# Rebuilding the opening of a fused graph-layer kernel: loads on one queue, a new product order, and the work around it moved

## The chip, the cores and the metric

The kernel runs on one core of one Trainium2 chip. The metric is the device time of one execution in microseconds (us); four executions of the kernel before lie within 1.4 us.

## The reference

For each of 64 batches of 256 tokens of width 768: a layer norm, then a graph layer over a 0/1 adjacency. In short (zero biases and the relation terms as in the full text):

```python
h    = max(layernorm(x), 0)                       # 64 x 256 x 768
adj  = heads.astype(float);  radj = adj.swapaxes(1, 2)
ctx  = (adj @ (h @ Wadj.T + badj)) / deg  + (radj @ (h @ Wrev.T + brev)) / rdeg
ctx += h @ Wself.T + bself
rel  = agg @ Wr.T + br*deg + ragg @ Wrr.T + brr*rdeg    # sums of relation embeddings
out  = x + ctx + rel
```

## The kernel before

A step t does the large products of batch M = t, the aggregates (adjacency times normalised tokens) of batch A = t+1, and the statistics and normalising of batch N = t+2. The products use a bilinear scheme with 15 products instead of 18: each is a sum of blocks of the left operand (made on POOL, GpSimd) times a sum of weight blocks (made once, on DVE, VectorE), and is added to one or more outputs. Several products accumulate in one PSUM bank (x, y, z, w), and DVE adds the bank into the output *in between*: so the next product of that bank must wait until DVE has read it.

```python
ORDER = (    # (product, bank, bias row, adds into x, left sums made on POOL just before)
    (11, "w", ...), (10, "z", ...), (3, "w", 1, ...), (2, "z", 0, ...), (5, "y", ...), (9, "x", ...),
    (7, "v", ...), (8, "y", ...), (6, "x", ...), (15, "u", ...), (14, "y", 2, ...), (12, "x", 4, ...),
    (4, "t", ...), (13, "y", 3, ...), (1, "x", 5, ...))
AHEAD = ("b2-a1", "a1+b1", "a2+b2")             # left sums made at the end of the step before

def normalise(b):                               # hx and lo on DVE, hi on ACT (ScalarE)
    ...
    for c in range(C):                          # C = 2 halves
        nc.vector.tensor_scalar(hx[:, c, :], s["x"][:, c, :], mean, 0.0, op0=ALU.subtract, op1=ALU.max)
        nc.scalar.activation(s["hi"][:, c, :], hx[:, c, :], AF.Copy, scale=rstd)
        nc.vector.scalar_tensor_tensor(s["lo"][:, c, :], hx[:, c, :], rstd, s["hi"][:, c, :], ...)

def step(t):
    M, A, N = t, t + 1, t + 2
    load(N)                                     # x, adj, xT of batch t+2, on SP's queue
    for k, (n, bank, row, reads, needs) in enumerate(ORDER):     # k: the "place" in the step
        for name in needs: combine_left(M, name)                 # POOL
        if t == 0 and k + 3 < len(ORDER): combine_weights(ORDER[k + 3][0])
        product(M, n, banks[bank], start, row)                   # PE (TensorE)
        for read in reads: add_out(M, banks[bank], *read)        # DVE
        if k in (1, 2, 3, 4, 5, 6): aggregate(A, k - 1)          # PE, then a multiply on DVE
        if k == 5: self_features(A)                              # POOL
        if k == 6: degrees(N); statistics(N)                     # ACT, DVE
        if k == 9: spread(N)
        if k == 11: normalise(N)
        if k == 13: store first half of out[M]
    for name in AHEAD: combine_left(A, name)                     # POOL
    store second half of out[M]
```

Each engine is given its instructions in the order of this loop, so "place" below always means: after the product with that number k, from 0 to 14, in this loop. (Cuts: reads and needs of ORDER, conditions at the ends.)

## Time and profile before

| | before |
|---|---|
| time, median (4 runs) | 2993.8 us |
| span of the profiled run | 2992.0 us, clock 0.994 |
| PE busy | 2911.9 us, 97% |
| first product of step 0 / of step 1 | 84.73 / 139.85 us |
| steps 1 to 62, apart | 45.25 us each |

PE is full from 140 us on. The prediction shows the lines for that.

### The profile page before, as it was taken

To read this page: it belongs to the slowest core of one execution; us is meant where nothing else is said; L and a number is where in the kernel's file an instruction comes from. 1 tells how busy PE (TensorE), PEld (TensorE's weight loads), DVE (VectorE), ACT (ScalarE), POOL (GpSimd) and SP (SyncE) were. 2 spreads that over 40 slices of the span, in tenths; PEclk is the share of its full clock that TensorE was granted. 3 is DMA by queue.
4 is the path that set the end of the run, shared out by engine and by line. 5 is a ranking of instruction groups with operands and counts; after the bars stand their busy time and mean duration, and the time that the engine had idled before them with its cause. 6 is when DMAs were issued, how large, how long until landed. Compare 5 with 4: busy or idle time off the path is not lost.

```text
span 2992.0 us, 33451 instructions
## 1 busy us (share of the span) xinstructions
PE 2911.9 (97%) x13514; PEld 2533.5 (85%) x13514; DVE 1243.4 (42%) x2530; ACT 355.3 (12%) x838; POOL 1779.5 (59%) x905
## 2 busy tenths in 40 slices
PE   2899999999999999999999999999999999999999
PEld 1688888888888888888888888888888888888887
DVE  3743434444444444443443444444444344444431
ACT  1111110110110111111111111111101101101100
POOL 2575565575565565665665665665755655755654
PEclk9899999999999999999999999999999999999999
DMA  7122222222222222122122122122122222222210
GB/s 233 63 72 74 88 68 75 78 72 79 74 75 81 71 77 81 64 85 81 64 82 84 64 76 91 64 74 92 64 74 84 71 75 76 73 81 74 75 64 22
DMA packets 126054, 233.27 MB, mean 78 GB/s; under 512 B 7092, under 2 KB 68276, under 8 KB 125896
## 3 DMA queue, kind: packets, MB, share of 16 engines
q1 hardware_dynamic: 114136, 219.28, 21.3%
q10 hardware_dynamic: 11760, 11.80, 1.3%
q8 instruction: 109, 1.79, 0.2%
q14 instruction: 49, 0.40, 0.0%
HBM read 180.46 MB, written 50.59 MB: 77 GB/s over the span
## 4 chain that ended last, share of the span: by engine, by line
PE 96%; DVE 1%; POOL 1%; ACTq 1%; DMA 1%; ACT 0%; issue 0%; SPq 0%; POOLq 0%
PE y L345 22%; PE x L345 22%; PE pa L319 12%; PE w L345 11%; PE z L345 11%; PE t L345 5%; PE u L345 5%; PE v L345 5%; ACTq L154 1%; POOL xT L310 1%; PE y L350 1%; PE x L350 0%; DVE w L180 0%; PE w L350 0%; PE z L350 0%; PE pt L272 0%
## 5 line engine op out<-in xcount | busy, mean ns | idle before, releaser
L340 POOL TENSOR_TENSOR b0+b<-X 128x768 f32<-128x768 f32 x64 | 118.2, 1847 | 736.7 <-PE z L345 736.7
L345 PE MATMUL y<-w,X 128*128 128x256 f32 x2304 | 530.8, 380 | 2.5 <-DVE x L358 2.5
L345 PEld LDWEIGHTS y<-w,X 128*128 128x128 f32 x2304 | 433.8, 190 | 66.9 <-DVE x L358 2.9
L310 POOL TENSOR_TENSOR xT<-xT,row 128x1536 f32<-128x1536 f32 x128 | 443.5, 3465 | 44.1 <-DMA row<-d 39.1
L319 PE MATMUL pa<-a,hi 128*128 128x512 f32 x768 | 352.4, 459 | 32.5 <-ACT hi L297 28.7
L340 POOL TENSOR_TENSOR X<-X 128x768 f32<-128x768 f32 x192 | 349.5, 1820 | 12.0 <-PE y L345 7.0
L345 PE MATMUL x<-w,X 128*128 128x256 f32 x1536 | 352.5, 379 | 0.0
L345 PE MATMUL x<-w,a2+b 128*128 128x256 f32 x1536 | 352.3, 379 | 0.0
L324 DVE TENSOR_TENSOR X<-pa,row 128x512 f32<-128x512 f32 x384 | 265.5, 692 | 187.4 <-PE pa L319 181.8
L345 PEld LDWEIGHTS x<-w,X 128*128 128x128 f32 x1536 | 287.0, 190 | 40.7
L345 PEld LDWEIGHTS x<-w,a2+b 128*128 128x128 f32 x1536 | 287.1, 190 | 38.1
L319 PE MATMUL pa<-a,lo 128*128 128x512 f32 x768 | 306.4, 399 | 0.5 <-DVE lo L298 0.5
L311 ACT ACTIVATE X<-xT 128x1536 f32<-128x1536 f32 x64 | 95.2, 1488 | 1599.2 <-POOL xT L310 1599.2
L340 POOL TENSOR_TENSOR a2+b<-X,a2+b 128x768 f32<-128x768 f32 x128 | 233.1, 1821 | 1.6 <-PE x L345 1.6
L319 PEld LDWEIGHTS pa<-a,hi 128*128 128x128 f32 x768 | 146.4, 191 | 61.3 <-ACT hi L297 29.6
L298 DVE SCALAR_TENSOR_TENSOR lo<-hx,cols,hi 128x768 fp32r<-128x768 f32 x128 | 130.4, 1019 | 161.7 <-ACT hi L297 161.7
L297 ACT ACTIVATE hi<-hx,cols 128x768 fp32r<-128x768 f32 x128 | 119.9, 937 | 563.3 <-DVE hx L294 563.3
L340 POOL TENSOR_TENSOR a2+b<-X 128x768 f32<-128x768 f32 x64 | 116.3, 1817 | 117.3 <-PE x L350 117.3
L340 POOL TENSOR_TENSOR a1+a<-X 128x768 f32<-128x768 f32 x64 | 116.9, 1826 | 106.8 <-PE w L350 106.8
L345 PE MATMUL w<-w,X 128*128 128x256 f32 x768 | 177.8, 381 | 0.0
L345 PE MATMUL w<-w,a1+b 128*128 128x256 f32 x768 | 176.3, 379 | 0.9 <-DVE x L360 0.9
L345 PE MATMUL t<-w,X 128*128 128x256 f32 x768 | 176.1, 379 | 0.7 <-DVE w L177 0.7
(84 smaller groups left out, 4008.7 us busy)
## 6 DMA issues: line engine op xcount, KB each, us to landing
x<-in_x_dram SPq DMA_DIRECT2D x64, 768.0 KB, 7.1
xT<-in_x_t_dram SPq DMA_DIRECT2D x64, 768.0 KB, 4.7
out_dram<-x SPq DMA_DIRECT2D x128, 384.0 KB, 3.1
adj<-in_adj_dram SPq DMA_DIRECT2D x64, 512.0 KB
row<-d SPq DMA_DIRECT2D x64, 512.0 KB
w<-in_Wself_dram ACTq DMA_DIRECT2D x6, 768.0 KB
w<-in_Wrev_dram ACTq DMA_DIRECT2D x5, 768.0 KB, 8.7
w<-in_Wadj_dram ACTq DMA_DIRECT2D x4, 768.0 KB, 10.3
```

What stands on the lines that cost most here:

```text
L154: nc.scalar.dma_start(W[n], v[:, :, ts(o, NB)])
L297: nc.scalar.activation(s["hi"][:, c, :], hx[:, c, :], AF.Copy, scale=rstd)
L298: nc.vector.scalar_tensor_tensor(s["lo"][:, c, :], hx[:, c, :], rstd, s["hi"][:, c, :].bitcast(F32), op0=ALU.mult, op1=ALU.subtract)
L310: nc.gpsimd.tensor_tensor(xT, xT, row[:, k : k + 1, :].to_broadcast([P, F, L]), op=op)
L311: nc.scalar.activation(s["X"][:, :, 2, :], xT, AF.Relu)
L319: nc.tensor.matmul(pa, s[part][:, c, ts(f, P)], s["a"][:, c, :, :].rearrange("p s i -> p (s i)"), start=(k == 0), stop=(k == 2 * C - 1),)
L324: nc.vector.tensor_mul(s["X"][:, f, 0:2, :].rearrange("p s i -> p (s i)"), pa, s["row"][:, 2:4, :].rearrange("p s i -> p (s i)"))
L340: nc.gpsimd.tensor_tensor(L[name], L[x], L[y], op=op)
L345: nc.tensor.matmul(ps, l[:, f, :], W[n][:, f, :], start=(start and f == 0), stop=(row is None and f == F - 1), skip_group_check=not start,)
L350: nc.tensor.matmul(ps, S[b]["tokT"], rows[:, row, :], start=False, stop=True, skip_group_check=not start)
```

## The change

Its intent is a shorter opening: weight loads leave ACT's queue for SP's and stand behind the token rows of batch 0; products whose weight operand is a single block come first, so they need no weight sum; the weight sums are spread over step 0; bias rows and half of a multiply move to other engines. To make room in step 0, all the work on batches A and N is now placed by one function with a delay of 8 places in step 0, 3 in step 1 and none from step 2 on. The core of the diff (cut: the new signs of PRODUCTS and LEFT, the bias rows, `load_rows`, and a third PSUM buffer for the ring that all banks but x and y share, which had two):

```diff
-AHEAD = ("b2-a1", "a1+b1", "a2+b2")
+AHEAD = ("b0+b1", "a1+a2", "a2+b2", "a0+a2", "a1+b1", "b1+b2")
 ORDER = (
-    (11, "w"), (10, "z"), (3, "w"), (2, "z"), (5, "y"), (9, "x"), (7, "v"), (8, "y"), (6, "x"), (15, "u"),
-    (14, "y"), (12, "x"), (4, "t"), (13, "y"), (1, "x"),
+    (5, "y"), (7, "v"), (9, "x"), (15, "u"), (10, "z"), (11, "w"), (2, "z"), (3, "w"), (8, "y"), (6, "x"),
+    (4, "t"), (14, "y"), (12, "x"), (13, "y"), (1, "x"),
 )
-                nc.scalar.dma_start(W[n], v[:, :, ts(o, NB)])
+                nc.sync.dma_start(W[n], v[:, :, ts(o, NB)])
+        def first_step(k):
+            ahead = {0: (11,), 1: (2,), 2: (3,), 3: (8,), 4: (6,), 5: (4,), 7: (13,), 9: (1,)}
+            for n in ahead.get(k, ()):
+                combine_weights(n, nc.vector)
+            ...                                  # statistics(1) at 5, normalise(1) at 6, spread(1) at 8
+        def others_of_step(A, N, k):
+            if N is not None and k == 0:
+                degrees(N)
+                statistics(N)
+            ...                                  # aggregate(A, k - 1) at 1 to 6, self_features(A) at 3
+                if k == 8:
+                    spread(N)
+                if k == 9:
+                    normalise(N)
         def step(t):
+            wait = {0: 8, 1: 3}.get(t, 0)
             for k, (n, bank, row, reads, needs) in enumerate(ORDER):
+                if t == 0:
+                    first_step(k)
                 product(M, n, banks[bank], start, row)
                 for read in reads:
                     add_out(M, banks[bank], *read)
-                if has_n and k == 6:
-                    degrees(N)
-                    statistics(N)
-                if has_n and k == 11:
-                    normalise(N)
+                for at in range(k, k + 1 if k + 1 < len(ORDER) else k + 4):
+                    others_of_step(A if has_a else None, N if has_n else None, at - wait)
```

(The tuples of ORDER are cut to product and bank here.) So in the steps from 2 on, statistics moved from place 6 to place 0, normalise from place 11 to place 9, and POOL makes six left sums at the end of a step instead of three.

More of the change, by code (lines that the diff above doesn't have):

```diff
@@ L25 @@
 PRODUCTS = {
+    5: ("b0+b1", "+10"),
+    7: ("a1+a2", "+22"),
+    9: ("a0+a2", "+20"),
+    15: ("b1+b2", "+11"),
+    10: ("b2-a1", "+22 -11"),
     11: ("a1", "-12 +22 +10"),
-    10: ("b2-a1", "+22 -11"),
+    2: ("a2+b2", "+21 -01 -22"),
     3: ("a1+b1", "+12 -02 -11"),
-    2: ("a2+b2", "+21 -01 -22"),
-    5: ("b0+b1", "-10"),
-    9: ("a0+a2", "-20"),
-    7: ("a1+a2", "+22"),
-    8: ("a1+b0+b1", "+10 -02"),
-    6: ("a0+a2+b2", "+20 -01"),
-    15: ("b1+b2", "+11"),
-    14: ("a0+a1+b0+b1", "+02"),
-    12: ("a0+a2+b0+b2", "+01"),
+    8: ("a1+b0+b1", "+02 -10"),
+    6: ("a0+a2+b2", "+01 -20"),
     4: ("b2", "+21 -11 -20"),
-    13: ("a0", "+00 -02 -20"),
-    1: ("b0", "+00 -01 -10"),
+    14: ("a0+a1+b0+b1", "-02"),
+    12: ("a0+a2+b0+b2", "-01"),
+    13: ("a0", "-00 +20 +02"),
+    1: ("b0", "-00 +10 +01"),
 }
 LEFT = {
-    "b2-a1": ("b2", ALU.subtract, "a1", "t1"),
-    "a1+b1": ("a1", ALU.add, "b1", "t2"),
-    "a2+b2": ("a2", ALU.add, "b2", "t0"),
-    "b0+b1": ("b0", ALU.add, "b1", "t1"),
-    "a1+a2": ("a1", ALU.add, "a2", "t2"),
-    "a0+a2": ("a0", ALU.add, "a2", "a2"),
+    "a1+a2": ("a1", ALU.add, "a2", "t1"),
+    "b0+b1": ("b0", ALU.add, "b1", "t2"),
+    "a2+b2": ("a2", ALU.add, "b2", "t0"),
+    "a0+a2": ("a0", ALU.add, "a2", "a2"),
+    "a1+b1": ("a1", ALU.add, "b1", "t3"),
+    "b1+b2": ("b1", ALU.add, "b2", "b1"),
+    "b2-a1": ("b2", ALU.subtract, "a1", "t1"),
     "a1+b0+b1": ("a1", ALU.add, "b0+b1", "a1"),
     "a0+a2+b2": ("a0", ALU.add, "a2+b2", "a2+b2"),
-    "b1+b2": ("b1", ALU.add, "b2", "b1"),
     "a0+a1+b0+b1": ("a0", ALU.add, "a1+b0+b1", "a1+b0+b1"),
@@ L55 @@
 }
-AHEAD = ("b2-a1", "a1+b1", "a2+b2")
-ROWS = ((0, 1, None), (1, 2, None), (0, 2, None), (0, 0, 2), (1, 1, None), (1, 0, 1))
+AHEAD = ("b0+b1", "a1+a2", "a2+b2", "a0+a2", "a1+b1", "b1+b2")
+ROWS = ((0, 1, None), (1, 2, None), (0, None, 2), (0, 2, 0), (1, None, 1), (1, 1, 0))
 ORDER = (
-    (11, "w", None, ((-1, 0, 2),), ()),
-    (10, "z", None, ((1, 1, 2),), ()),
-    (3, "w", 1, ((1, 1, 2),), ("b0+b1",)),
-    (2, "z", 0, ((1, 0, 1),), ("a1+a2",)),
-    (5, "y", None, ((-1, 1, 0),), ("a0+a2",)),
-    (9, "x", None, ((-1, 0, 0),), ("a1+b0+b1", "a0+a2+b2")),
-    (7, "v", None, ((1, 0, 1, 2),), ("b1+b2",)),
-    (8, "y", None, ((-1, 1, 2),), ()),
-    (6, "x", None, ((-1, 0, 1),), ("a0+a1+b0+b1",)),
-    (15, "u", None, ((1, 1, 1, 2),), ("a0+a2+b0+b2",)),
-    (14, "y", 2, ((1, 0, 2),), ()),
-    (12, "x", 4, ((1, 1, 1),), ()),
-    (4, "t", None, ((-1, 0, 1), (1, 1, 1)), ()),
-    (13, "y", 3, ((1, 0, 0),), ()),
-    (1, "x", 5, ((1, 1, 0),), ()),
+    (5, "y", None, ((1, 1, 0),), ()),
+    (7, "v", None, ((1, 0, 1, 2),), ()),
+    (9, "x", None, ((1, 0, 0),), ("b2-a1",)),
+    (15, "u", None, ((1, 1, 1, 2),), ()),
+    (10, "z", None, ((1, 1, 2),), ()),
+    (11, "w", None, ((-1, 0, 2),), ()),
+    (2, "z", 0, ((1, 0, 1),), ("a1+b0+b1",)),
+    (3, "w", 1, ((1, 1, 2),), ("a0+a2+b2",)),
+    (8, "y", None, ((1, 1, 2),), ()),
+    (6, "x", None, ((1, 0, 1),), ("a0+a1+b0+b1",)),
+    (4, "t", None, ((-1, 0, 1), (1, 1, 1)), ("a0+a2+b0+b2",)),
+    (14, "y", 2, ((-1, 0, 2),), ()),
+    (12, "x", 4, ((-1, 1, 1),), ()),
+    (13, "y", 3, ((-1, 0, 0),), ()),
+    (1, "x", 5, ((-1, 1, 0),), ()),
 )
@@ L141, in main_path @@
         dram = main.enter_context(tc.tile_pool(name="dram", bufs=3, space=bass.MemoryType.DRAM))
+        ps3 = main.enter_context(tc.tile_pool(name="ps3", bufs=3, space=bass.MemoryType.PSUM))
         ps2 = main.enter_context(tc.tile_pool(name="ps2", bufs=2, space=bass.MemoryType.PSUM))
@@ L148, in main_path, with load_weights @@
         cols = [pool1.tile([P, C, 64], F32, name=f"cols{i}") for i in range(2)]
-        def load_weights():
-            for n, (_, right) in PRODUCTS.items():
+        def load_weights(products):
+            for n in products:
+                right = PRODUCTS[n][1]
                 k, o = int(right[1]), int(right[2])
                 v = (wadj_t, wrev_t, wself_t)[k].rearrange("(f p) o -> p f o", p=P)
-                nc.scalar.dma_start(W[n], v[:, :, ts(o, NB)])
+                nc.sync.dma_start(W[n], v[:, :, ts(o, NB)])
         single = {right[1:]: n for n, (_, right) in PRODUCTS.items() if len(right) == 3}
@@ L163, in turn, with combine_weights @@
                 turned.add(n)
-        def combine_weights(n):
+        def combine_weights(n, eng):
             first, *others = PRODUCTS[n][1].split()
@@ L174, in combine_weights @@
                     if first[0] == "-" and k == 0:
-                        nc.vector.tensor_sub(W[n], W[m], W[n])
+                        eng.tensor_tensor(W[n], W[m], W[n], op=ALU.subtract)
                     else:
-                        nc.vector.tensor_add(W[n], W[n], W[m])
+                        eng.tensor_tensor(W[n], W[n], W[m], op=ALU.add)
                 else:
                     assert first[0] == "+" or k > 0
-                    nc.vector.tensor_sub(W[n], W[n], W[m])
+                    eng.tensor_tensor(W[n], W[n], W[m], op=ALU.subtract)
         R = {}
         def load_rows():
-            R["eT"] = pool1.tile([P, NREL], F32, name="eT")
-            nc.sync.dma_start(R["eT"], e_t)
-            R["wr"] = [pool1.tile([P, H], F32, tag=f"t{k}", name=f"wr{k}") for k in range(2)]
-            nc.sync.dma_start(R["wr"][0], wr_t)
-            nc.sync.dma_start(R["wr"][1], wrr_t)
-            brow = R["brow"] = pool3.tile([P, H], F32, tag="x", name="brow")
-            nc.gpsimd.memset(brow, 0.0)
-            pick = R["pick"] = pool1.tile([P, 2, P], F32, tag="t2", name="pick")
-            nc.gpsimd.memset(pick, 0.0)
-            R["full"] = pool2.tile([P, len(ROWS), NB], F32, tag="X", name="rows_full")
-            nc.gpsimd.memset(R["full"], 0.0)
+            sizes = {"full": len(ROWS) * NB, "brow": H, "pick": 2 * P, "wr0": H, "wr1": H, "eT": NREL}
+            work = pool2.tile([P, sum(sizes.values())], F32, tag="X", name="rows_work")
+            at = 0
+            for n, size in sizes.items():
+                R[n] = work[:, at : at + size]
+                at += size
+            nc.gpsimd.memset(work[:, : at - 2 * H - NREL], 0.0)
+            R["full"] = R["full"].rearrange("p (k n) -> p k n", n=NB)
+            R["pick"] = R["pick"].rearrange("p (k n) -> p k n", n=P)
+            brow = R["brow"]
+            nc.sync.dma_start(R["eT"], e_t)
+            nc.sync.dma_start(R["wr0"], wr_t)
+            nc.sync.dma_start(R["wr1"], wrr_t)
             for q in range(4):
@@ L199, in prepare_rows @@
         def prepare_rows():
-            eT, wr, brow, pick, full = (R[n] for n in ("eT", "wr", "brow", "pick", "full"))
+            eT, brow, pick = (R[n] for n in ("eT", "brow", "pick"))
+            wr = R["wr0"], R["wr1"]
             for k, at in ((0, 1), (1, NBASE + 1)):
                 to = pick[:, k, :].rearrange("p (q r) -> p q r", q=4)[:, :, 3 + k]
-                nc.vector.tensor_copy(to, eT[:, at : at + 1].to_broadcast([P, 4]))
+                nc.scalar.activation(to, eT[:, at : at + 1].to_broadcast([P, 4]), AF.Copy)
             for n in range(2):
@@ L210, in prepare_rows, with place_rows @@
                 nc.vector.tensor_add(brow[:, ts(n, HO)], brow[:, ts(n, HO)], pr[:, :HO])
+        def place_rows():
+            brow, full = R["brow"], R["full"]
             hi = pool1.tile([P, len(ROWS), NB], F32R, tag="hx", name="rows_hi")
@@ L215, in prepare_rows @@
                     if of == c and minus is None:
-                        nc.vector.tensor_copy(full[at, k, :], brow[at, ts(plus, NB)])
+                        nc.scalar.activation(full[at, k, :], brow[at, ts(plus, NB)], AF.Copy)
+                    elif of == c and plus is None:
+                        nc.scalar.activation(full[at, k, :], brow[at, ts(minus, NB)], AF.Copy, scale=-1.0)
                     elif of == c:
-                        nc.vector.tensor_sub(full[at, k, :], brow[at, ts(plus, NB)], brow[at, ts(minus, NB)])
+                        nc.gpsimd.tensor_tensor(
+                            full[at, k, :], brow[at, ts(plus, NB)], brow[at, ts(minus, NB)], op=ALU.subtract
+                        )
             nc.scalar.activation(hi, full, AF.Copy)
-            nc.vector.tensor_sub(rows, full, hi.bitcast(F32))
+            nc.gpsimd.tensor_tensor(rows, full, hi.bitcast(F32), op=ALU.subtract)
             for q in (0, 2):
@@ L232, in load, with load_xt @@
             nc.sync.dma_start(s["adj"], adj_v[b])
+        def load_xt(b):
+            s = S[b]
             s["xT"] = pool1.tile([P, F, L], F32, tag="xT", name=f"xT_{b}")
@@ L308, in self_features @@
             xT, row = s["xT"], s["row"]
-            for k, op in ((0, ALU.subtract), (1, ALU.mult)):
-                nc.gpsimd.tensor_tensor(xT, xT, row[:, k : k + 1, :].to_broadcast([P, F, L]), op=op)
+            parts = ((nc.gpsimd, 0, F),) if b > 0 else ((nc.gpsimd, 0, F // 2), (nc.vector, F // 2, F))
+            for eng, f0, f1 in parts:
+                for k, op in ((0, ALU.subtract), (1, ALU.mult)):
+                    v = xT[:, f0:f1, :]
+                    eng.tensor_tensor(v, v, row[:, k : k + 1, :].to_broadcast([P, f1 - f0, L]), op=op)
             nc.scalar.activation(s["X"][:, :, 2, :], xT, AF.Relu)
@@ L330, in left_blocks, with combine_left @@
             S[b]["L"] = {f"{'ab'[c]}{k}": X[:, :, k, ts(c, P)] for c in range(C) for k in range(3)}
-        def combine_left(b, name):
+        def combine_left(b, name, eng=None):
             x, op, y, home = LEFT[name]
@@ L339, in combine_left @@
                 L[name] = pool1.tile([P, F, P], F32, tag=home, name=f"{name}_{b}")
-            nc.gpsimd.tensor_tensor(L[name], L[x], L[y], op=op)
+            (eng or nc.gpsimd).tensor_tensor(L[name], L[x], L[y], op=op)
         def product(b, n, ps, start, row=None):
@@ L369, in start @@
         def start():
+            order = [n for n, *_ in ORDER]
+            order.remove(12)
+            order.remove(14)
+            order[6:6] = (12, 14)
             load(0)
-            load_rows()
+            load_xt(0)
+            load_weights(order[:2])
             degrees(0)
-            load_weights()
             statistics(0)
             spread(0)
+            load_rows()
+            load_weights(order[2:6])
+            load(1)
+            load_weights(order[6:])
             normalise(0)
-            load(1)
             new_left(0)
@@ L382, in start @@
                 aggregate(0, f)
+            prepare_rows()
             left_blocks(0)
-            for name in AHEAD:
-                combine_left(0, name)
-            combine_weights(ORDER[0][0])
-            prepare_rows()
-            for k in (1, 2):
-                combine_weights(ORDER[k][0])
-            degrees(1)
-            statistics(1)
-            spread(1)
-            normalise(1)
+            for k, name in enumerate(AHEAD):
+                combine_left(0, name, nc.vector if k % 2 else nc.gpsimd)
+            load_xt(1)
+            combine_weights(10, nc.vector)
+        def first_step(k):
+            if k == 0:
+                turn(12)
+                turn(14)
+            ahead = {0: (11,), 1: (2,), 2: (3,), 3: (8,), 4: (6,), 5: (4,), 7: (13,), 9: (1,)}
+            for n in ahead.get(k, ()):
+                combine_weights(n, nc.vector)
+            if k == 2:
+                place_rows()
+            if k == 5:
+                degrees(1)
+                statistics(1)
+            if k == 6:
+                normalise(1)
+            if k == 8:
+                spread(1)
+        def others_of_step(A, N, k):
+            if N is not None and k == 0:
+                degrees(N)
+                statistics(N)
+            if A is not None:
+                if k == 1:
+                    new_left(A)
+                if 1 <= k <= F:
+                    aggregate(A, k - 1)
+                if k == 3:
+                    self_features(A)
+                    if N is not None:
+                        load_xt(N)
+            if N is not None:
+                if k == 8:
+                    spread(N)
+                if k == 9:
+                    normalise(N)
         def step(t):
@@ L398, in step @@
             has_a, has_n = A < B, N < B
+            wait = {0: 8, 1: 3}.get(t, 0)
             if has_n:
                 load(N)
-            if has_a:
-                new_left(A)
             banks = {}
@@ L406, in step @@
                     combine_left(M, name)
-                if t == 0 and k + 3 < len(ORDER):
-                    combine_weights(ORDER[k + 3][0])
+                if t == 0:
+                    first_step(k)
                 start = bank not in banks
                 if start:
-                    pool, tag = (ps1, bank) if bank in ("x", "y") else (ps2, "q")
+                    pool, tag = (ps1, bank) if bank in ("x", "y") else (ps3, "q")
                     banks[bank] = pool.tile([P, 512], F32, tag=tag, name=f"{bank}_{M}")[:, :NB]
@@ L415, in step @@
                     add_out(M, banks[bank], *read)
-                if has_a and k in (1, 2, 3, 4, 5, 6):
-                    aggregate(A, k - 1)
-                if has_a and k == 5:
-                    self_features(A)
-                if has_n and k == 6:
-                    degrees(N)
-                    statistics(N)
-                if has_n and k == 9:
-                    spread(N)
-                if has_n and k == 11:
-                    normalise(N)
+                for at in range(k, k + 1 if k + 1 < len(ORDER) else k + 4):
+                    others_of_step(A if has_a else None, N if has_n else None, at - wait)
                 if t == B - 1 and k == 2:
@@ L435, in step @@
             nc.sync.dma_start(out_v[M][:, 1, :], S[M]["x"][:, 1, :])
+        nc.scalar.activation(half[:, :1], half[:, :1], AF.Copy)
         for i in range(2):
```

## The prediction

> **What bounds the kernel now.** I first read the page's busy row and its 40 slices (tenths; a slice is 74.8 us).
>
> ```profile
> PE 2911.9 (97%) x13514; PEld 2533.5 (85%) x13514; DVE 1243.4 (42%) x2530; ACT 355.3 (12%) x838; POOL 1779.5 (59%) x905
> PE   2899999999999999999999999999999999999999
> ```
>
> PE is the bound in every slice but the first two; it idles 2992.0 - 2911.9 = 80 us in all. The windows view says where (columns: stretch, length, busy time and instructions of each engine, clock, DMA share, GB/s).
>
> ```profile
> 0.00:20.00 20.00, 0.45 (x1) 0.18 (x1) 4.53 (x20) 2.99 (x9) 4.03 (x10) 1.00 0.96 305
> 20.00:40.00 20.00, 0.80 (x1) 0.29 (x1) 0.83 (x1) 1.27 (x3) 0.00 (x0) 1.00 1.09 348
> ...
> 1000.00:2900.00 1900.00, 1900.00 (x8862) 1657.39 (x8861) 790.22 (x1638) 227.56 (x546) 1161.35 (x588) 1.00 0.22 76
> ```
>
> From 140 us on PE never waits, and the steps start 45.25 us apart (step 1 at 139.85, step 63 at 2945.05, 62 steps between). So only two things can change the time: when step 1 starts, and whether a later step loses its gapless PE. The timeline of the opening shows the first.
>
> ```profile
> 33.44 4.38 ACTq L154 DMA_DIRECT2D w<-in_Wadj_dram  x2
> 37.87 0.28 ACT L274 ACTIVATE tokT<-pt 128x128 fp32r<-128x128 f32 x1 [27.87 <-DMA w<-in_Wadj_dram]
> 43.28 0.35 SPq L281 DMA_DIRECT2D row<-d  x1
> 48.35 1.29 DVE L324 TENSOR_TENSOR X<-pa,row 128x512 f32<-128x512 f32 x2 [5.61 <-DMA row<-d]
> 84.73 4.52 PE L345 MATMUL w<-w,X 128*128 128x256 f32 x12
> 139.85 2.75 PE L345 MATMUL w<-w,X 128*128 128x256 f32 x12
> ```
>
> ACT issues 15 weight loads, 2.17 us each once the transfers back up (4.38 for these two), and can do nothing else until 37.87; the row broadcast lands at 48.35, the first product starts at 84.73. Step 0 then takes 139.85 - 84.73 = 55.1 us, 10 above a normal step.
>
> **What the Trainium skill says.** (1) "TensorE: Matmul & The Clock Gate", Terms and first table: ACT and DVE are strict FIFO. The trace agrees: ready work on ACT sat 27.87 us behind issues. (2) "SBUF — State Buffer", "SBUF: two separate sides": a DVE operation with two SBUF inputs and a GpSimd operation that reads SBUF lock each other out for whole instructions. It agrees: a 128x1536 weight sum on DVE takes 1.75 us alone and 2.78 and 3.25 beside POOL; POOL's 1.83 sums become 3.32 and 3.35 there. (3) "DMA: Bandwidth & Descriptors", "Issuing engines are not separate DMA queues": issuing elsewhere saves sequencer time, not transfer time. It agrees: the opening moves about 348 GB/s, and a 768 KB load takes 2.17 us of that whoever issues it.
>
> **The change, opening.** All weight loads move to SP's queue, only two of them ahead of the row round trip. Ahead of it then go x, adj, xT and two weights, 3.7 MB or 10.5 us at 348 GB/s. x and adj still land at 5.6 and 7.0. The table load moves off the path (1.3 us): columns ready 9.4 instead of 10.6, transposed and copied by 10.3, d issued at 10.3. d's data come behind the two weights, so I put its landing at 14 and that of the row (about 4 us) at 18: 30 us earlier than 48.35.
>
> From the row to the first product, before: 7.8 us to the last aggregate product on DVE, then weight sums, bias rows and the statistics of batch 1, all ahead of it: 36.4 us. After: half of the 7 us of xT work goes to DVE. Through the lock the halves alternate, 2 x 0.9 + 2 x 1.75 = 5.3 us, so DVE reaches its six aggregate multiplies at about 22 and ends them at 29. Two bias products on PE (8 instructions, 0.32 us each warm, 4.9 us in all at half clock as before) end at 31. Product 5 needs only b0+b1 (1.83 on POOL) and an unsummed weight. **First product: 31 instead of 84.7.**
>
> **The change, step 0.** It does not run at PE's pace. The 14 weight sums left are 14 x 1.76 = 24.6 us of DVE; two statistics 2 x 3.6; batch 1's normalise 5.2; ten adds into x 4.0: 41 us in program order on DVE before the first aggregate multiply of batch 1, from about 41 us (after the left and weight sums of the start) to 82, and with the lock (the same row of sums cost before 3.8 us extra) to about 87. PE stops on it: product 2 writes bank z, which is free only after an add standing behind the sums for 2, 3, 8 and 6; product 3 likewise behind the sums for 4 and the statistics. The third aggregate of batch 1 waits for the first multiply, at 87. From there 4 x 0.93 + 3 x 2.7 = 11.8 us of PE, a multiply and a first left sum (2.8): **step 1 starts at about 102 instead of 139.85, a gain of 38 us**. The 53.7 us gained at the first product shrink since step 0 now takes 71 us, not 55. The ideal would be 31 + 45 = 76.
>
> **The change, every later step.** Here something moves that the title does not name. From step 2 on, the statistics of batch t+2 stand at product 0 instead of product 6 of DVE's program, and their x is only asked for at the start of the same step, when the buffer's old content is stored. In the step at 999.56:
>
> ```profile
> 1000.20 0.34 SPq L435 DMA_DIRECT2D out_dram<-x  x1
> 1003.04 0.39 SPq L230 DMA_DIRECT2D x<-in_x_dram  x1
> 1024.30 1.01 DVE L252 BATCH_NORM_STATS2 stats<-x 128x6 f32<-128x384 f32 x2
> 1027.83 0.41 DVE L360 TENSOR_TENSOR x<-x,y 128x256 f32<-128x256 f32 x1
> ```
>
> The landing records of all steps put x at 4.2 to 4.8 us after its issue, median 4.45; before, the statistics came long after. In the new kernel the first half is stored earlier (DVE has no normalise at the end of the step), so the second store lands 2.4 instead of 2.8 us after its issue: x issued at step + 3.0, landed at + 7.45. DVE, idle from + 2.8, then runs the statistics (3.53 from 1024.30 to 1027.83), an add (0.6) and the first aggregate multiply (0.69): + 12.35. PE comes to the third aggregate, which needs that buffer (two pa buffers), at 4 x 2.59 + 2 x 0.93 = 12.2, or 12.0 as the profile draws it. **So PE loses about 0.25 us in each of the 60 steps 2 to 61: 15 us.** The left sum b2-a1, now behind the square root on POOL, is ready at 7.45 + 3.7 + 1.85 = 13.0 and wanted at 13.1: hidden, barely. The other products are the same in number and shape, so a gapless step stays 45.25.
>
> Sum: 2993.7 - 38 + 15 = **2971 us**.
>
> **Rivals.** (a) *Statistics early are free*: if x lands 0.3 us sooner than I think, the step stays 45.25 and the time is about 2956. For it: the margin is smaller than the spread of landings. Against: the adj operand lands 1.3 us after x and its four ACT reads take 1.7, so the chain has no slack either. (b) *The early statistics become a real stall*: should stores or loads be slower in the new order, each microsecond costs 60 us; at 1.5 us a step the time is about 3045. Against it: the queue is otherwise empty then and transfers ran at 400 GB/s. (c) *DVE doesn't hold step 0 back*: if PE ran step 0 at its pace, step 1 would start near 80 and, with no stall later, 2934 us. Against it: 14 sums in one order before the reads that free the banks. (d) *The lock makes it worse*: DVE and POOL fully in series in step 0 (POOL has some 14 us of sums and row work there) put step 1 at about 112 and the time at 2981.
>
> **Range and chances.** Step 1 between 90 and 112 gives 28 to 50 us of gain; the stall 0 to 35 us in all. Together 2948 to 2998 eight times in ten. Faster by over 2% needs under 2933.8, which even (c) does not reach: 0.04. Slower by over 2% needs over 3053.6, (b) at more than 1.6 us a step: 0.04. Within 2%: 0.92.
>
> **What would show it.** Right: the first product near 31 and step 1 near 102; in PE's waits, one or two of 5 to 10 us on DVE's adds into x in step 0, and pa on the multiply X some 60 times for about 15 us; in DVE's waits, statistics on the load of x about 60 times, 4 to 5 us each (280 us in all, nearly all harmless); product groups of the same mean, 380 ns. Wrong: steps 45.25 apart after step 2 (then rival a); or 46.5 and more apart (b); step 1 before 85 (c); or a PE wait on a weight load, which I count as absent since the last weight should land by 55.

## More of the kernel before

Timeline of the kernel before (start, duration in us, engine, line, operation, out<-in; rows left out):

```profile
1034.28 0.42 DVE L358 TENSOR_TENSOR x<-x,y 128x256 f32<-128x256 f32 x1 [2.13 <-PE y L350]
...
1037.33 1.88 DVE L294 TENSOR_SCALAR hx<-x,cols 128x768 f32<-128x768 f32 x1
...
1039.38 2.75 PE L345 MATMUL y<-w,X 128*128 128x256 f32 x12
...
1041.23 0.61 DVE L294 TENSOR_SCALAR hx<-x,cols 128x768 f32<-128x768 f32 x1
1042.85 1.02 DVE L298 SCALAR_TENSOR_TENSOR lo<-hx,cols,hi 128x768 fp32r<-128x768 f32 x1 [1.00 <-ACT hi L297]
1043.79 0.41 DVE L360 TENSOR_TENSOR x<-x,t 128x256 f32<-128x256 f32 x1
1044.12 0.41 DVE L358 TENSOR_TENSOR x<-x,t 128x256 f32<-128x256 f32 x1
1044.45 0.41 DVE L358 TENSOR_TENSOR x<-x,y 128x256 f32<-128x256 f32 x1
1044.80 2.54 PE L345 MATMUL w<-w,X 128*128 128x256 f32 x11
```

DVE's add of product 14 (x<-x,y at 1034.28) is done before normalise begins at 1037.33, so product 13, which takes bank y again at 1039.38, never waits. Three adds pile up behind normalise, which takes 6.5 us, but nobody needs them soon: the next step begins with product 11 in bank w.

## The result

The changed kernel takes 3142.5 us (median of 4 runs, 3136.5 to 3156.0) against 2993.8: a ratio of 1.050, interval 1.047 to 1.054, so slower by 5%. Ratios here are the mean time of one kernel's runs over that of the other's of the same rounds, so not quite the ratio of the medians quoted. The prediction said 2971, and 2948 to 2998 eight times in ten.

The opening went as predicted. Timeline of the changed kernel, rows of the opening: the multiplies that wait for the broadcast row, the first product, and the first product of step 1.

```profile
18.13 3.43 DVE L328 TENSOR_TENSOR xT<-xT,row 128x768 f32<-128x768 f32 x2 [1.97 <-DMA row<-d]
30.44 2.86 PE L363 MATMUL y<-w,b0+b 128*128 128x256 f32 x12
...
105.57 2.86 PE L363 MATMUL y<-w,b0+b 128*128 128x256 f32 x12 [2.86 <-POOL b0+b L358]
```

The row landed at 18 (predicted 18), the first product began at 30.4 (predicted 31, before 84.7), step 1 at 105.6 (predicted 102, before 139.85): 34.3 us gained where 38 were predicted.

Everything after that went wrong. From step 1 to step 62 the kernel before takes 2899.91 - 139.85 = 2760.1 us and the changed one 3045.68 - 105.57 = 2940.1: 180.0 us more over 61 steps, 2.95 each. With the opening, 180.0 - 34.3 = 145.7; the spans differ by 145.0. Where PE waits, in the waits view of the changed kernel (waiter <- releaser: us in total, times, longest):

```profile
PE y L363 <- DVE x L378: 124.0, 61, 4.4
PE pa L337 <- DVE X L342: 19.1, 25, 3.5
...
PE w L363 <- DVE x L376: 7.8, 1, 7.8
```

The second line is the wait that I had predicted (15 us, for the early statistics). The first, six times as large, I had not. It is one wait of 2.0 us in each step. The loads of PE's weights, which the trace keeps apart as PEld, show it as 2.3 us:

```profile
PEld y L363 <- DVE x L378: 137.8, 60, 2.3
```

The timeline of a step shows it:

```profile
1009.70 1.80 POOL L358 TENSOR_TENSOR a2+b<-X,a2+b 128x768 f32<-128x768 f32 x1 [0.90 <-PE x L363]
1009.93 1.99 DVE L309 TENSOR_SCALAR hx<-x,cols 128x768 f32<-128x768 f32 x1
1011.47 2.12 POOL L358 TENSOR_TENSOR b0+b<-X 128x768 f32<-128x768 f32 x1
1011.98 2.75 PE L363 MATMUL y<-w,X 128*128 128x256 f32 x12
...
1013.07 1.34 DVE L313 SCALAR_TENSOR_TENSOR lo<-hx,cols,hi 128x768 fp32r<-128x768 f32 x1 [1.15 <-ACT hi L312]
1013.55 2.52 POOL L358 TENSOR_TENSOR a1+a<-X 128x768 f32<-128x768 f32 x1
1014.33 2.16 DVE L309 TENSOR_SCALAR hx<-x,cols 128x768 f32<-128x768 f32 x1
...
1019.10 0.42 DVE L378 TENSOR_TENSOR x<-x,y 128x256 f32<-128x256 f32 x1
...
1019.56 2.46 PEld L363 LDWEIGHTS y<-w,X 128*128 128x128 f32 x12 [2.31 <-DVE x L378]
1019.57 2.86 PE L363 MATMUL y<-w,X 128*128 128x256 f32 x12 [2.00 <-DVE x L378]
```

Product 14 fills bank y from 1011.98 to 1014.9. Normalise, now at place 9, has begun at 1009.93, two places before product 14, and DVE can add product 14 into the output only behind it, at 1019.10. Product 13 wants bank y at 1017.6 and gets it at 1019.57. And normalise takes 8.5 us (1009.93 to 1018.43) instead of 6.5, because sums on POOL run beside it, the first of the six among them: hx, 0.61 us alone, takes 1.99 and 2.16.

So the theory after the result (**A, order and lock**): normalise stands ahead of an add that PE needs within 8 us, *and* the lock between DVE and POOL makes it long enough to matter. Its rival (**B**, the prediction's rival b): the early statistics, waiting for x, are what the steps lose to. A third (**C**): the new product order or POOL's load as such, without the block on DVE.

### The profile page after: what moved, and what is told of

Same layout as the page of the kernel before. It is cut to its first block, busy times and chain, and to the rows that moved or that the text cites. A ratio compares the mean times of both kernels' runs of the same rounds, so it can differ in the third digit from the quotient of the medians.

```text
span 3137.0 us, 33335 instructions
## 1 busy us (share of the span) xinstructions
PE 2951.0 (94%) x13514; PEld 2535.8 (81%) x13514; DVE 1344.4 (43%) x2526; ACT 362.9 (12%) x845; POOL 1891.5 (60%) x903
## 4 chain that ended last, share of the span: by engine, by line
PE 66%; DVE 21%; DMA 7%; ACT 4%; issue 1%; POOL 1%; SPq 0%; DVEq 0%; ACTq 0%; POOLq 0%
PE y L363 14%; PE x L363 14%; PE w L363 11%; PE z L363 10%; PE pa L337 10%; DVE hx L309 8%; DVE lo L313 5%; DMA x<-in_x_dram 4%; ACT hi L312 4%; PE u L363 3%; PE v L363 3%; DMA out_dram<-x 2%; DVE x L376 2%; DVE x L378 2%; DVE stats L267 2%
## 5 line engine op out<-in xcount | busy, mean ns | idle before, releaser
L363 PE MATMUL y<-w,X 128*128 128x256 f32 x2304 | 545.1, 387 | 124.0 <-DVE x L378 119.6
L363 PEld LDWEIGHTS y<-w,X 128*128 128x128 f32 x2304 | 434.4, 193 | 200.1 <-DVE x L378 137.8
L270 POOL TENSOR_TENSOR cols<-cols,half 128x2 f32<-128x2 f32 x64 | 68.5, 1070 | 633.4 <-DVE cols L269 622.8
L328 POOL TENSOR_TENSOR xT<-xT,row 128x1536 f32<-128x1536 f32 (+1 forms) x128 | 440.0, 3437 | 12.1 <-DMA row<-d 7.1
L337 PE MATMUL pa<-a,hi 128*128 128x512 f32 x768 | 358.8, 467 | 23.2 <-DVE X L342 19.1
L309 DVE TENSOR_SCALAR hx<-x,cols 128x768 f32<-128x768 f32 x128 | 261.0, 2039 | 0.0
L267 DVE BATCH_NORM_STATS2 stats<-x 128x6 f32<-128x384 f32 x256 | 127.1, 538 | 270.9 <-DMA x<-in_x_dram 270.9
L257 ACT ACTIVATE a<-adj 128x256 fp32r<-128x256 int32 x256 | 103.5, 406 | 1011.8 <-DMA adj<-in_adj_dram 1011.8
L358 POOL TENSOR_TENSOR a2+b<-X 128x768 f32<-128x768 f32 x64 | 162.4, 2538 | 96.3 <-PE x L368 96.3
L313 DVE SCALAR_TENSOR_TENSOR lo<-hx,cols,hi 128x768 fp32r<-128x768 f32 x128 | 152.1, 1188 | 137.4 <-ACT hi L312 137.4
L363 PE MATMUL y<-w,b0+b 128*128 128x256 f32 x768 | 178.2, 382 | 7.2 <-DVE x L378 4.4
L363 PE MATMUL z<-w,a2+b 128*128 128x256 f32 x768 | 177.9, 382 | 2.9 <-DVE x L376 2.9
```

The lines of the kernel that those rows point to most:

```text
L257: nc.scalar.activation(s["a"][:, c, k, :], s["adj"][:, c, k, :], AF.Copy, accum_out=tok[b % 2][:, c, 4 - k : 5 - k])
L267: nc.vector.bn_stats(stats[:, c, n, :], s["x"][:, c, ts(n, HO)])
L270: nc.gpsimd.tensor_tensor(v[:, :, RSTD], v[:, :, RSTD], half, op=ALU.pow)
L309: nc.vector.tensor_scalar(hx[:, c, :], s["x"][:, c, :], v[:, c, MEAN : MEAN + 1], 0.0, op0=ALU.subtract, op1=ALU.max)
L328: eng.tensor_tensor(v, v, row[:, k : k + 1, :].to_broadcast([P, f1 - f0, L]), op=op)
L337: nc.tensor.matmul(pa, s[part][:, c, ts(f, P)], s["a"][:, c, :, :].rearrange("p s i -> p (s i)"), start=(k == 0), stop=(k == 2 * C - 1),)
```

## The experiments

Eleven kernels, all correct, each timed in three rounds with the kernel before on the same chip (its medians 2993.3, 2993.5 and 2993.8). Changes in a step hold from step 2 on unless said otherwise; the new order of POOL's sums holds in every step.

### a_norm11: normalise where it was before, place 11

```diff
-                if k == 9:
+                if k == (9 if t < 2 else 11):
                     normalise(N)
```

> The changed kernel with one move: from step 2 on, normalise stands after product 11 of the order (the twelfth) instead of after product 9 (the tenth). Theory A (order and lock): in the changed kernel PE waits 2.0 us a step for product 13, whose bank y is freed by DVE's add of product 14, which stands behind an 8.5 us normalise. Here that add comes before normalise, so the 2.0 us wait must vanish (about 120 us in all, time about 3020). But normalise then stands ahead of the add of product 13, and bank y is taken again by product 5 of the next step: if POOL's sums still stretch normalise to 8 us, a wait of up to 1.3 us a step appears at product 5 (time up to 3100). Rival B (early statistics: the x load): the time stays within 15 us of the changed kernel's.

Measured: **3230.8 us**, slower still (ratio 1.080). The wait for bank y is gone, and another has come:

```profile
PE x L363 <- DVE x L378: 161.7, 60, 2.7
PE pa L337 <- DVE X L342: 17.8, 19, 3.7
```

The timeline of a step has this row:

```profile
1103.05 4.46 PE L363 MATMUL x<-w,X 128*128 128x256 f32 x12 [2.69 <-DVE x L378]
```

In the new order place 11 is product 14, not product 12 as before the change. Normalise at place 11 lets the add of product 14 pass and blocks that of product 12, which frees bank x for product 1: 2.7 us a step. The wait alone does not make this kernel slower than the changed one. At the weight loads it is 179.8 us in all against 137.8, 42 more, where the profiled runs lie 94.7 apart. The rest fits the clock that PE was granted: it was half for 136.5 us between step 1 and step 62, in 34 stretches, against 20.5 us in 6. Half of the difference, 58 us, is my estimate of the loss; the product in the row above, 2.75 us long elsewhere, took 4.46. I had named the next step's product 5 as the place of a new wait, and was wrong about which bank; that a place number taken over from another order means another thing is the lesson. For theory A it speaks: the wait follows normalise about. B is out as the main cause: the statistics were not touched.

### a_stats6: only the statistics back to place 6

```diff
-            if N is not None and k == 0:
+            if N is not None and k == (0 if t < 2 else 6):
                 degrees(N)
                 statistics(N)
```

> The changed kernel with one move: from step 2 on, the statistics of batch t+2 stand at product 6 (as before the change) instead of product 0. Theory A: the 2.0 us wait of product 13 stays, and only the waits of the third aggregate product on DVE go (19 us in the waits view, some 20 to 45 us with what the pipelined matmuls hide): 3095 to 3125. Rival B: the late x is what the steps lose most to, so the step falls to 45.3 us and the time to 2960 to 2990.

Measured: **3121.2 us**, 21 less than the changed kernel. The waits of PE on the multiply X fall from 19.1 to 3.4 us, that for bank y stays at 124.3. So the early statistics cost some 21 us here, near the 15 predicted; B fails.

### a_both: both moves

The two diffs above together:

```diff
-            if N is not None and k == 0:
+            if N is not None and k == (0 if t < 2 else 6):
-                if k == 9:
+                if k == (9 if t < 2 else 11):
```

> Both moves together: statistics at product 6 and normalise after product 11, from step 2 on. If the two together are the whole loss, and no new wait at product 5 takes its place, the steps are 45.25 us apart again and only the opening's gain stands: 2994 - 34 = 2960. With the wait at product 5 that the lock would make: 2960 to 3040. If something else of the change slows the steps (rival C: the new product order or POOL's sums themselves), it stays over 3040 with waits of PE on POOL.

Measured: **3169.6 us**, with 158.0 us of waits for bank x. The two moves together do not cure it, for the reason seen in a_norm11. No wait of PE on POOL worth naming appeared, which leaves C without support.

### a_ahead: only POOL's sums reordered

```diff
+AHEAD_LATER = ("a2+b2", "b0+b1", "a1+a2", "a0+a2", "a1+b1", "b1+b2")
-                for name in AHEAD:
+                for name in AHEAD_LATER:
                     combine_left(A, name)
```

a2+b2 reuses the buffer of a sum that product 12 reads, so POOL, put to it first, is silent until product 12 is done.

> The changed kernel with only the order of POOL's six left sums at the end of a step altered: a2+b2 first, which must wait for product 12, so that POOL is silent while DVE normalises; normalise stays after product 9 and the statistics at product 0. Theory A with the lock as its half: hx falls from a mean of 2.04 us towards 0.6 to 1.3, normalise from 8.5 to about 6.5, and the 2.0 us wait of product 13 to 0.3 or less: time 3020 to 3060. If the order alone makes the wait and the lock does not matter, the wait stays near 2 us and the time near 3140. Rival B: no change either.

Measured: **3028.6 us**: 114 us less, though DVE's program is not altered in a single place. Its timeline:

```profile
1022.15 2.00 DVE L310 TENSOR_SCALAR hx<-x,cols 128x768 f32<-128x768 f32 x1
1026.23 0.61 DVE L310 TENSOR_SCALAR hx<-x,cols 128x768 f32<-128x768 f32 x1
1027.85 1.02 DVE L314 SCALAR_TENSOR_TENSOR lo<-hx,cols,hi 128x768 fp32r<-128x768 f32 x1 [1.00 <-ACT hi L313]
1029.44 0.41 DVE L379 TENSOR_TENSOR x<-x,y 128x256 f32<-128x256 f32 x1
1029.84 1.80 POOL L359 TENSOR_TENSOR a2+b<-X 128x768 f32<-128x768 f32 x1 [6.11 <-PE x L369]
1029.91 2.46 PEld L364 LDWEIGHTS y<-w,X 128*128 128x128 f32 x12 [0.44 <-DVE x L379]
```

The second hx takes 0.61 us, normalise 6.6 (1022.15 to 1028.78). The 2.0 us waits for bank y have left PE's list, and at the weight loads 0.44 of 2.31 us is left (26.1 us in 60 steps). Only the first hx is still long, beside one sum that POOL had already begun. The lock, then, is a necessary part of the cause: with the same order of DVE's instructions and 6.6 us of normalise, PE gets bank y almost in time.

### a_norm7: normalise two places earlier

```diff
-                if k == 9:
+                if k == (9 if t < 2 else 7):
                     normalise(N)
```

> The changed kernel with one move the other way: from step 2 on, normalise stands after product 3 of the order (place 7) instead of place 9; POOL's sums as in the changed kernel. Theory A: normalise now starts some 5 us earlier, ends before product 14 is done, and no add that PE needs within 8 us stands behind it. The 2.0 us wait for bank y must go and, unlike with place 11, no wait for bank x may come in its place: about 3142 - 125 = 3010 to 3030, with the 20 us of waits on the third aggregate product left. If any place of normalise costs the same because DVE is short of time, it stays over 3100.

Measured: **3055.6 us**; the 2.0 us wait is gone, but more stays than expected, with a line

```profile
PE y L363 <- DVE x L376: 40.2, 60, 0.9
```

Normalise at place 7 now stands ahead of the add of product 8, and product 14 wants bank y after it: up to 0.9 us a step. Same mechanism, another pair of products. So with products 8, 14 and 13 in one bank, none of the three places tried, 7, 9 and 11, is free of such a wait for a whole normalise; 8, 10 and those after 11 were not run.

### c_ahead_stats6: reordered sums and late statistics

On top of a_ahead:

```diff
-            if N is not None and k == 0:
+            if N is not None and k == (0 if t < 2 else 6):
```

> POOL's end-of-step sums reordered (a2+b2 first) and the statistics back at place 6, both from step 2 on; normalise stays at place 9. If the two shown causes are all, what is left of the 3028 us of the reordered one is the stats part, 20 to 50 us: 2975 to 3005, with steps 45.3 to 45.7 us apart. If the steps stay near 46.5, a third cause is still there.

Measured: **2986.1 us** (ratio 0.998): steps 45.56 us apart, each within 0.02 of that from step 3 on. It is 42 us under a_ahead, so the same move of the statistics is worth 42 us here and was worth 21 in a_stats6; the clock has a share in that. Taking off half of the half-clock time between step 1 and step 62 (an estimate; 20.5 and 37.5 us in the first pair, 13.7 and 6.8 in this one), the profiled runs give 27 and 36 us, and the pair a_norm11 and a_both (136.5 and 68.3 us) 30. The 0.44 us wait at the weight loads stays here too (22.4 us in 60 steps).

### c_ahead_stats3_norm7 and c_reads_first

The first has POOL's sums reordered, statistics at place 3 and normalise at place 7 (on top of a_ahead):

```diff
-            if N is not None and k == 0:
+            if N is not None and k == (0 if t < 2 else 3):
-                if k == 9:
+                if k == (9 if t < 1 else 7):
```

The second adds, in step 0 only, that each weight sum stands behind the add of its place instead of ahead of the product:

```diff
-            for n in ahead.get(k, ()):          # in first_step, ahead of the product
-                combine_weights(n, nc.vector)
+                if t == 0:                      # after the adds of this place
+                    sums_of_first_step(k)
```

> POOL's sums reordered, the statistics at place 3 (x has landed by then) and normalise at place 7, where POOL is mostly silent. Nothing that PE waits for should stand behind either: steps 45.25 apart, only the opening's gain left, 2994 - 34 = 2960 (2955 to 2970); it would beat both kernels. Steps over 45.5 apart would mean a cause not found.

> As the one before, and in step 0 each weight sum is put behind the add of its product instead of ahead of it, so that the adds that free the banks no longer wait for it. My account of step 0 says that DVE's amount of work sets the start of step 1, not the order of the adds: PE's waits on DVE's adds in step 0 (7.8, 2.9 and 2.7 us) shrink or go, but step 1 starts within 3 us of before (105) and the time changes by less than 4 us. If instead the blocked banks are what holds step 0, step 1 starts 8 to 13 us earlier.

Measured: **3015.6** and **3015.4 us**. The first missed its 2960: steps are 46.12 apart, with 39.9 us of waits for bank y, the trap of a_norm7 again, which I had not yet seen when I wrote the expectation. The second started step 1 when it was expected to, but did not free the banks. PE's waits on DVE's adds in the first 108 us, in the former and then in the latter (there the two of bank w are 1.0 and 0.9):

```profile
PE w L364 <- DVE x L377: 8.1, 1, 8.1
PE w L364 <- DVE x L379: 2.7, 1, 2.7
PE z L364 <- DVE x L377: 2.6, 1, 2.6
```

```profile
PE z L364 <- DVE x L377: 9.8, 1, 9.8
```

Most of the wait only moved from bank w to bank z, and step 1 starts at 105.8 instead of 106.6. In the changed kernel DVE is busy 55.8 of the 60 us from 30 to 90 (windows view), which fits the prediction's account that the amount of work sets step 0. But as the banks stayed blocked, this run does not tell that account from one in which the blocked banks set it.

### a_split: normalise in two halves

```diff
-                if k == 9:
+                if t == 0 and k == 9:
                     normalise(N)
+                if t > 0 and at_product == 9:
+                    normalise(N, (0,))
+                if t > 0 and at_product == 11:
+                    normalise(N, (1,))
```

> The changed kernel with normalise cut in two from step 1 on: its first half after product 6 (place 9, as in the change), its second after product 14 (place 11). POOL's order and the early statistics stay. Theory A: a half takes 4.5 us beside POOL's sums and 8.0 us lie between the end of place 9 and the first use of bank y, so the add of product 14 comes in time; behind the second half stands the add of product 12, wanted by product 1 some 5.4 us after place 11: just in time. So nearly all of the 2.0 us goes: 3005 to 3035, with the stats part left. If only silence on POOL can cure it, it stays over 3080.

Measured: **2996.3 us** (ratio 1.002), 146 us under the changed kernel, with POOL's order and the early statistics untouched. No wait for a bank is left in the steps, and the normal step is 2.26 us shorter than the changed kernel's (45.49 and 47.75, medians), as much as the wait was at the weight loads; 23.1 us on the multiply X (21 waits) are. So the cure works from DVE's side alone too: a block of work ahead of an add is harmless when it is shorter than the time until the bank is wanted.

### c_split: halves, reordered sums, late statistics

The diff of a_split on top of c_ahead_stats6.

> Normalise cut in two (places 9 and 11) from step 1 on, POOL's end-of-step sums reordered and the statistics at place 6 from step 2 on. With all the named causes away the steps are 45.25 us apart (45.56 with the reordering and the statistics alone) and only the opening's gain is left: 2960 to 2970, faster than both kernels. A step still over 45.4 would mean a cause not found.

Measured: **2958.8 us** (2958.0 to 2960.0), ratio 0.988, interval 0.987 to 0.990: 35 us under the kernel before, clear of noise though under 2%, and faster than all others. Steps are 45.22 us apart from step 2 on, and its first page row shows PE full:

```profile
PE 2913.9 (99%) x13514; PEld 2535.5 (86%) x13514; DVE 1246.9 (42%) x2526; ACT 356.0 (12%) x845; POOL 1787.9 (60%) x903
```

The new opening, freed of what came with it, is worth some 33 us (step 1 at 107.18 instead of 139.85). And C is out: the new order and all six of POOL's sums are here, and the steps are as short as before. They are 0.34 us shorter than in c_ahead_stats6, about as much as its wait at the weight loads.

### b_stats0: the kernel before with early statistics alone

```diff
-                if has_n and k == 6:
+                if has_n and k == (6 if t < 2 else 0):
                     degrees(N)
                     statistics(N)
```

> The kernel before with one thing of the change alone: from step 2 on, the statistics of batch t+2 at place 0 instead of 6. It measures what the early statistics cost by themselves. x lands some 7.8 us into the step there; the statistics, an add and the multiply end 4.9 us later at 12.7, and PE wants the third aggregate's buffer at 12.0 to 12.2: 0.5 to 0.9 us a step, 30 to 55 us in all, 3025 to 3050. Rival B (the early statistics are the main loss of the change) wants 120 us or more here.

Measured: **3186.3 us** (ratio 1.066), worse than the change itself. My expectation was wrong by the same oversight as the prediction: I looked only at the aggregates' buffers. Timeline of one step:

```profile
1002.77 2.75 PE L345 MATMUL z<-w,b2-a 128*128 128x256 f32 x12
1008.20 1.02 DVE L252 BATCH_NORM_STATS2 stats<-x 128x6 f32<-128x384 f32 x2 [4.81 <-DMA x<-in_x_dram]
...
1011.73 0.41 DVE L358 TENSOR_TENSOR x<-x,z 128x256 f32<-128x256 f32 x1
...
1012.29 2.83 PE L345 MATMUL z<-w,a2+b 128*128 128x256 f32 x12 [2.21 <-DVE x L358]
```

In the old order product 2 takes bank z three places in, and the add of product 10 that frees it stands behind the statistics: 154.1 us of waits. In the new order the first five products go to five different buffers (y, x and three of the ring for v, u and z), which may be why early statistics cost it only 20 to 40 us; no run took order and buffers apart. So this does not rescue rival B for the change, where the same move costs 21 to 42 us: what an early wait on DVE costs depends on the adds that stand behind it.

## Why the prediction was wrong

- **Bounds.** Right: only the start of step 1 and the gapless later steps could change the time.
- **Opening.** Right in each number: row 18 (18 measured), first product 31 (30.4), step 1 at 102 (105.6). Its term was 38 us and measured 34.3. (One reading was slightly off: ACT sat idle for 27.87 us, but the operand it was to copy was only there at 11.15, so ready work sat for 26.7.) PE's waits in step 0 on adds were foreseen in kind: those named, at products 2 and 3, took 2.9 and 2.7 us, and the longest, 7.8, came at product 11, which was not named. That DVE's amount of work sets step 0 fits the runs, but is not separated from the blocked banks.
- **Early statistics.** Right in mechanism: the statistics wait for x in 61 places for 270.9 us in all (280 predicted). The loss was 21 us (a_stats6) to 42 (c_ahead_stats6 against a_ahead) where the term said 15; so the term was too small. Its sum has a slip (7.45 + 3.53 + 0.6 + 0.69 is 12.27, not 12.35), which works the other way.
- **"The other products are the same in number and shape, so a gapless step stays 45.25."** This step failed: from step 3 on the steps are 48.09 us in the mean. I asked of each later step only what the moved statistics do to the aggregates' buffers. I had seen that normalise moves from the end of the step, and booked it as a gain (an earlier store), without asking which adds now stand behind it: the add of product 14, awaited by product 13 through bank y. And I had written down the lock between DVE and POOL, with its numbers, but for DVE operations with two SBUF inputs, and used it for step 0 only. hx reads a single tensor and is held all the same, 1.99 and 2.16 us instead of 0.61; in every later step sums on POOL now fall beside normalise and stretch it from 6.5 to 8.5 us.
- **The missing term.** The wait for bank y, 137.8 us at the weight loads in 60 steps, is the main part of the 180. The rest: the early statistics, 27 to 36 with the clock's share taken off; step 1, 52.8 us long, 7.6 above the normal step; and PE's clock, which fell to half for one 3.41 us window in six of the later steps after such waits, 6 x 1.7 = 10 us. That makes 182 to 191, so the sum closes to some 10 us. That runs of the changed kernel spread over 20 us, with mean clocks from 0.993 to 0.989, fits the clock's share, but is not separately tested.
- **Range.** Rival (b) had a stall of 1.5 us a step or more, but by another cause, a late x. It was given 4% because I asked only whether transfers might be slow.

## What to carry to other kernels

When work is moved in an in-order engine's program, list every instruction that now stands *behind* it and what waits for each, in every phase of the kernel, not only where the change aims. A block is free only if it is shorter than the time until the first such result is wanted, with its length taken as it will be beside its new neighbours on the other engines; if it is too long, cut it in two or silence the neighbour. A place number in a schedule has to be worked out again when the order changes.

## What the Trainium skill lacked or had wrong

- "TensorE: Matmul & The Clock Gate", "HAM oscillation — how this bites in real kernels", gives as the abstract rule no PE idle gaps over about 3.4 us. Here a gap of 2.0 us once a step was sometimes enough. Between the first products of step 1 and of step 62 the changed kernel has six half-clock windows of 3.41 us, five of them just after a gap of 2.0 us and one after 4.4; a_norm11, with gaps of 2.7 us, has 34 stretches of 3.41 or 6.83 us; the kernel before and c_split have none. A product in such a window, right after a gap of 2.0 us, took 4.54 instead of 2.86 us.
- "SBUF — State Buffer", "Who interferes with whom", says that the loser of the lock fully blocks. The runs agree, and add what the page does not say: the time blocked shows as the instruction's own busy time, so hx has a mean of 2.04 us in the changed kernel, 1.32 with POOL reordered, and 0.61 alone; and POOL's 1.80 us sums become 2.1 to 2.6 in the same stretch.
- "DMA: Bandwidth & Descriptors", "Anatomy of one DMA — SWDGE (gpsimd) path", has a fit of 2.0 us plus bytes over 436 GB/s for the other path, 3.8 us for the 768 KB of x. x is issued from SP's queue, with adj's 512 KB right behind it, and the statistics that wait for it began 4.2 to 4.8 us after the issue in 55 of 60 steps of the changed kernel. The page has no fit for that path; as the two loads ran together, this is no clean measure of one.
